# A graph network's output layer: own features through the adjacency's diagonal, division by degree behind the dense product

## The chip, the cores and the metric

The kernel runs on one core of one Trainium2 chip. The metric is the device time of one execution in microseconds. Engines: PE multiplies matrices, DVE is the vector engine, ACT the scalar engine, POOL is GpSimd, SP here only issues DMA.

## The reference, cut to what matters

Four graph layers over x (2708 x 512, fp32) with one adjacency matrix. The third layer multiplies by the adjacency three times ("hops"). The change concerns the end of the third hop and the fourth layer:

```python
deg = max((adj != 0).sum(-1), 1)
...
# fourth layer; node_degree = deg, so dinv * a_hat * dinv divides each row by deg
a_hat  = adj + eye(n)
a_norm = dinv * a_hat * dinv
pooled = a_norm @ x + x
x = layernorm(x + relu(pooled @ W + b))
```

In other words pooled = (adj @ x + x) / deg + x, which equals (adj + diag(1 + deg)) @ x / deg. The division acts on rows and can wait until after the multiplication by W.

## The kernel before

Each hop and the output layer are a "sweep": two ranges of columns, in each seven second-level Strassen products (Q1 to Q7), in each again seven chains of matmuls. DVE forms the sums of adjacency tiles, `comb`, and of features, `tsum`, and adds each finished chain to its result, `leave`. `at(position, f)` puts an action in a list that is sorted by position; the compiled order follows this list only roughly. In the traces a wait at one instruction of POOL holds back those behind it on that engine: POOL starts a layernorm's power at 2876.21 us, 3.67 us after DVE has its input ready (2872.54), behind three DMA issues, the first of them after an idle time of 2.29 us.

```python
for o, x, y, op_, pos in (("s3", (0,0), (1,0), ALU.subtract, -0.5), ((1,0), (1,0), (1,1), ALU.add, 0.6), ...):
    for k in range(nk):                               # sums of adjacency tiles z
        at(b + u * (pos + 0.8 * k / nk), lambda a=(o, x, y, op_, k), f=comb: f(*a))
...
def sums(g):                                          # new features, before the next sweep
    ...
    nc.vector.tensor_tensor(t["T1"], t["T3"], t["B11"], ALU.subtract)
    nc.vector.tensor_tensor(t["T2"], t["B22"], t["T1"], ALU.subtract)
    nc.vector.tensor_tensor(t["T3"], t["B22"], t["T3"], ALU.subtract)
    nc.vector.tensor_tensor(t["T4"], t["B21"], t["T2"], ALU.subtract)
```

At the end of the third hop each row tile is turned to natural layout (four transposes, `ps_n`), normalized and stored, then transposed back (four more, `ps_t`) and stored a second time as X3T:

```python
def b(...):                                           # done5, per row tile
    ps = untranspose2(cc, s, lo, w)
    got["x"] = y = nat("o")
    layernorm([(y, 0, D)], ps, w, True)
    store2(X3, y, h, r0, w)
def c(...):
    store_T(X3T[g, h, s][:, lo : lo + w], transposed([(got["x"], 0, D)], w)[:, :, :w])
```

The output layer loads X3T and a row of 1/deg, and prepares the sum before the dense product:

```python
def pre(s, c):                                        # done6
    nc.vector.tensor_tensor(y, y, t, ALU.add)         # adj @ x + x
    nc.vector.tensor_tensor(y, y, row[g, h, s], ALU.mult)
    nc.vector.tensor_tensor(y, y, t, ALU.add)
...
px = dense(lambda c: cc(s, c)[:, lo : lo + w], W[6], w)
nc.vector.tensor_tensor(px[:w], px[:w], vec[6][:w], ALU.add)
```

The layernorm takes its power on POOL, between two small DVE instructions. In the trace of this kernel, loads that POOL has to issue first delay that power, and DVE stands still behind it (3.84 us in the line shown below).

## Time and profile before

| | |
|---|---|
| time, median of 3 | 2920.15 us (2917.83 to 2923.89) |
| span of the profiled execution | 2921.0 us |
| PE busy | 98% |
| DVE busy | 77% |
| PE's waits from 2430 us on | 12 us, every one for DVE |

The prediction reads these and shows the lines. One more is worth having, of DVE's timeline near the end of the kernel before (start, duration, engine, line, operation, and in brackets the idle time before it and what ended it):

```profile
2876.81 0.15 DVE L555 SCALAR_TENSOR_TENSOR rstd<-mv,rstd 83x1 f32<-83x1 f32 x1 [3.84 <-POOL rstd L553]
```

DVE stands for 3.84 us behind a power on POOL, and PE's hole at 2878.70 follows.

### The profile page before, as it was taken

To read this page: it belongs to the slowest core of one execution; us is meant where nothing else is said; L and a number is where in the kernel's file an instruction comes from. 1 tells how busy PE (TensorE), PEld (TensorE's weight loads), DVE (VectorE), ACT (ScalarE), POOL (GpSimd) and SP (SyncE) were. 2 spreads that over 40 slices of the span, in tenths; PEclk is the share of its full clock that TensorE was granted. 3 is DMA by queue.
4 is the path that set the end of the run, shared out by engine and by line. 5 is a ranking of instruction groups with operands and counts; after the bars stand their busy time and mean duration, and the time that the engine had idled before them with its cause. 6 is when DMAs were issued, how large, how long until landed. Compare 5 with 4: busy or idle time off the path is not lost. (4 is left out here: it accounts for less than half of the span.)

```text
span 2921.0 us, 37394 instructions
## 1 busy us (share of the span) xinstructions
PE 2863.3 (98%) x10846; PEld 1847.0 (63%) x10846; DVE 2235.8 (77%) x5676; ACT 579.0 (20%) x1133; POOL 658.2 (23%) x1178
## 2 busy tenths in 40 slices
PE   7999999999999999999999999999999999999998
PEld 5655665557665656766666666666666666655664
DVE  5898697566638675875789788887888878689887
ACT  4644200101137454651100000000000200100001
POOL 0123224213310101123113033030330413512202
PEclk9999999999999999999999999999999999999999
DMA  7666466445634333665677777576775776966653
GB/s 224 190 211 182 135 212 215 132 154 160 186 107 140 115 114 99 174 190 154 204 203 223 202 206 234 156 217 196 218 223 149 225 204 181 262 164 179 181 162 89
DMA packets 376248, 523.96 MB, mean 179 GB/s; under 512 B 64454, under 2 KB 326640, under 8 KB 376044
## 3 DMA queue, kind: packets, MB, share of 16 engines
q1 hardware_dynamic: 307128, 372.01, 44.4%
q0 software_dynamic: 53376, 139.76, 15.0%
q10 hardware_dynamic: 15540, 9.82, 1.2%
q8 instruction: 86, 1.41, 0.2%
q14 instruction: 118, 0.97, 0.1%
HBM read 432.14 MB, written 89.21 MB: 178 GB/s over the span
## 5 line engine op out<-in xcount | busy, mean ns | idle before, releaser
L1114 DVE TENSOR_TENSOR z<-z 128x339 f32<-128x339 f32 (+1 forms) x966 | 457.0, 504 | 14.8 <-PE accu L1154 3.6
L1172 ACT COPY q<-accu 128x338 f32<-128x338 f32 (+1 forms) x84 | 34.5, 443 | 983.0 <-PE accu L1154 983.0
L1154 PE MATMUL accu<-z,t 128*128 128x338 f32 (+1 forms) x644 | 196.0, 451 | 6.5 <-DVE q L1178 3.5
L1154 PE MATMUL accc<-s,t 128*128 128x338 f32 (+1 forms) x644 | 198.4, 451 | 1.1 <-DVE s L1114 1.1
L1154 PE MATMUL accd<-z,t 128*128 128x338 f32 (+1 forms) x644 | 193.8, 448 | 2.3 <-DVE z L1114 2.3
L1154 PE MATMUL accc<-z,t 128*128 128x338 f32 (+1 forms) x644 | 194.4, 448 | 0.0
L553 POOL TENSOR_TENSOR rstd<-rstd,neg_half 128x1 f32<-128x1 f32 (+3 forms) x92 | 62.1, 675 | 577.7 <-DVE rstd L552 574.7
L1275 POOL DMA_DIRECT2D Y<-y x192 | 104.8, 552 | 372.2 <-DVE y L1270 341.6
L396 DVE TENSOR_TENSOR a<-a,a 128x384 f32<-128x384 f32 (+2 forms) x330 | 161.2, 509 | 16.2 <-PE accu L451 15.7
L1154 PEld LDWEIGHTS accu<-z,t 128*128 128x128 f32 x644 | 122.5, 192 | 68.7 <-DVE q L1178 4.0
L1154 PEld LDWEIGHTS accd<-z,t 128*128 128x128 f32 x644 | 122.2, 190 | 63.5 <-DVE z L1114 2.9
L1154 PEld LDWEIGHTS accc<-s,t 128*128 128x128 f32 x644 | 120.7, 191 | 65.4 <-issue 8.7
L1154 PEld LDWEIGHTS accc<-z,t 128*128 128x128 f32 x644 | 121.9, 190 | 60.7 <-issue 2.1
L1114 DVE TENSOR_TENSOR s<-z 128x338 f32<-128x338 f32 (+1 forms) x322 | 150.2, 504 | 10.6 <-PE accc L1154 7.1
L1178 DVE TENSOR_TENSOR q<-q,accd 128x338 f32<-128x338 f32 (+1 forms) x112 | 56.3, 502 | 128.4 <-PE accd L1154 128.4
L972 ACT ACTIVATE e<-row,neg_s 128x384 f32<-128x384 f32 (+5 forms) x176 | 100.4, 570 | 79.8 <-DVE e L974 24.6
L974 DVE TENSOR_TENSOR e<-e,f 128x384 f32<-128x384 f32 (+5 forms) x176 | 87.3, 504 | 31.1 <-ACT f L973 30.5
L973 ACT ACTIVATE f<-row,neg_s 128x384 f32<-128x384 f32 (+5 forms) x176 | 100.0, 568 | 25.4 <-PE accc L451 5.1
L599 PE MATMUL ps_d<-w,q 128*128 128x512 f32 (+2 forms) x192 | 85.9, 595 | 1.4 <-DVE ld L1360 1.3
L890 DVE SCALAR_TENSOR_TENSOR deg<-a,deg 128x384 f32<-128x384 f32 (+2 forms) x152 | 75.2, 503 | 14.0 <-DMA a<-in_adjT 12.7
L399 POOL DMA_DIRECT2D As<-a x120 | 64.6, 542 | 92.9 <-DVE a L396 77.4
L975 DVE SCALAR_TENSOR_TENSOR a<-a,e 128x384 f32<-128x384 f32 (+2 forms) x160 | 79.9, 505 | 4.2 <-DMA a<-in_adjT 2.2
(609 smaller groups left out, 5933.8 us busy)
## 6 DMA issues: line engine op xcount, KB each, us to landing
z<-As SPq DMA_DIRECT2D x320, 169.5 KB
z<-As SPq DMA_DIRECT2D x320, 169.0 KB
a<-in_adjT SPq DMA_DIRECT2D x240, 192.0 KB
z<-in_adjT SPq DMA_DIRECT2D x240, 169.5 KB
z<-in_adjT SPq DMA_DIRECT2D x240, 169.0 KB
a<-in_adjT SPq DMA_DIRECT2D x120, 165.0 KB
a<-in_adjT SPq DMA_DIRECT2D x112, 128.0 KB
As<-a POOLq DMA_DIRECT2D x60, 192.0 KB, 3.3
```

The costliest lines, as they stand in the source:

```text
L396: nc.vector.tensor_tensor(A[r, dst, k][:, :n], A[r, a, k][:, :n], A[r, b, k][:, :n], op)
L399: nc.gpsimd.dma_start(out=SD[m][k * P : (k + 1) * P, R0 : R0 + n], in_=A[r, dst, k][:, :n])
L553: nc.gpsimd.tensor_tensor(rstd[:w, 1:2], rstd[:w, 0:1], neg_half[:w], ALU.pow)
L599: nc.tensor.matmul(o, lhs(c), r, start=c == 0 and n == 0, stop=c == DC - 1, skip_group_check=True)
L890: nc.vector.scalar_tensor_tensor(d[:w, :n], a[:w, :n], 0.0, d[:w, :n], ALU.not_equal, ALU.add)
L972: nc.scalar.activation(e[:w, :n], row[R0, h][0][:w, :n], AF.Exp, bias=neg_s[:w, t : t + 1])
L973: nc.scalar.activation(f[:w, :n], row[R0, h][1][:w, :n], AF.Exp, bias=neg_s01[:w, t : t + 1])
L974: nc.vector.tensor_tensor(e[:w, :n], e[:w, :n], f[:w, :n], ALU.min)
L975: nc.vector.scalar_tensor_tensor(a[:w, :n], a[:w, :n], 0.0, e[:w, :n], ALU.not_equal, ALU.mult)
L1114: nc.vector.tensor_tensor(d[:, :n], Z[x + (k,)][:, :n], Z[y + (k,)][:, :n], op)
L1154: nc.tensor.matmul(B[home][:, :n], stat(v, k), a[:, :n], start=bool(start and k == 0), stop=k == nk - 1, skip_group_check=True)
L1275: nc.gpsimd.dma_start(out=rows[:, :, f * P : (f + 1) * P], in_=o[32 * f : 32 * (f + 1), : m * P].rearrange("p (b d) -> p b d", d=P))
```

## The change

The intent: don't make, store, load and add the transposed features. Add 1 + deg to the diagonal of the adjacency tiles as they pass through DVE, and divide by deg in the instruction that adds the bias. Cut to its core:

```diff
+    diag = const.tile([P, 4, KT], F32, name="diag")          # 1 + deg, and differences for Strassen's sums
+    rdeg_f = const.tile([P, 24], F32, name="rdeg_f")          # 1/deg by row tile
...
+                def add_diag(p, q, k, ...):
+                    r0, c0 = (q * K2 + k) * P, i0 + p * n
+                    lo, hi = max(r0, c0), min(r0 + P, c0 + n)
+                    if lo < hi:
+                        z = Z[p, q, k][:, lo - c0 : hi - c0]
+                        nc.vector.scalar_tensor_tensor(z, ident[:, lo - r0 : hi - r0], diag[:, d, ...], z,
+                                                       ALU.mult, ALU.add)
+                for p, q, pos in ((0, 0, -0.52), (1, 0, -0.51), (1, 1, 0.59), (0, 1, 4.04)):
+                    for k in range(nk) if on_diag and op != "12" else ():
+                        at(b + u * (pos + 0.8 * k / nk), ...add_diag...)
...   # done5
-            def c(s=s, lo=lo, w=w, got=got):
-                store_T(X3T[g, h, s][:, lo : lo + w], transposed([(got["x"], 0, D)], w)[:, :, :w])
...   # a few small instructions; 16 small loads and one transpose bring 1/deg into rdeg_f
...   # done6: rows(), load_x3T() and pre() removed
-                nc.vector.tensor_tensor(px[:w], px[:w], vec[6][:w], ALU.add)
+                nc.vector.scalar_tensor_tensor(px[:w], px[:w], rdeg_f[:w, r : r + 1], vec[6][:w], ALU.mult, ALU.add)
-            p = p0 - 0.095 + 0.14 * i if end else p0 + 0.4 + 0.25 * i
+            p = p0 - 0.095 + 0.14 * i if end else p0 + 0.1 + 0.28 * i
-    sweep2(S[6], 0, done6)
+    sweep2(S[6], 0, done6, True)
```

More of the change, by code (lines that the diff above doesn't have):

```diff
@@ L102, in gnn_kernel @@
     nc.vector.memset(rdeg, 1.0)
+    diag = const.tile([P, 4, KT], F32, name="diag")
+    nc.vector.memset(diag, 1.0)
+    diag_r = const.tile([P, 3], F32, name="diag_r")
+    nc.vector.memset(diag_r, 0.0)
+    rdeg_f = const.tile([P, 24], F32, name="rdeg_f")
     wab_sb = const.tile([P, 2 * DC, 2], F32, name="wab_sb")
@@ L130, in gnn_kernel @@
            for g, (_, n) in enumerate(RANGES2) for h in range(2)}
-    X3T = {(g, h, s): dram.tile([D, n], F32, name=f"X3T{g}_{h}{s}", tag=f"X3T{g}_{h}{s}")
-           for g, (_, n) in enumerate(RANGES2) for h in range(2) for s in range(2)}
     SUMS = ("s1", "s2", "s3", "s4")
@@ L908, in end @@
                 nc.vector.tensor_scalar(o, ps[:wq, i : i + 1], 1.0, None, ALU.max)
+                nc.vector.tensor_scalar(diag[:wq, h, q : q + 1], o, 1.0, None, ALU.add)
                 nc.vector.reciprocal(o, o)
@@ L1081, in ext_sums, with tiles2, sweep2 @@
             nc.gpsimd.dma_start(out=SE[m, g, s][q * P : (q + 1) * P, :], in_=E[o][:, :n])
-    def sweep2(base, ext, done, extra=None):
+    def tiles2(n):
+        return [(s, lo, min(P, n - lo)) for s in range(2) for lo in range(0, n, P)]
+    def sweep2(base, ext, done, on_diag=False):
         nk = K2 + ext
@@ L1120, in sweep2, with add_diag @@
                         at(b + u * (pos + 0.8 * k / nk), lambda a=(o, x, y, op_, k), f=comb: f(*a))
+                def add_diag(p, q, k, op=op, Z=Z, i0=i0, n=n):
+                    r0, c0 = (q * K2 + k) * P, i0 + p * n
+                    lo, hi = max(r0, c0), min(r0 + P, c0 + n)
+                    if lo < hi:
+                        z = Z[p, q, k][:, lo - c0 : hi - c0]
+                        d = {"11": 0, "22": 1, "s1": 1, "s2": 2, "s3": 0, "s4": 3}[op]
+                        nc.vector.scalar_tensor_tensor(z, ident[:, lo - r0 : hi - r0], diag[:, d, r0 // P : r0 // P + 1],
+                                                       z, ALU.mult, ALU.add)
+                for p, q, pos in ((0, 0, -0.52), (1, 0, -0.51), (1, 1, 0.59), (0, 1, 4.04)):
+                    for k in range(nk) if on_diag and op != "12" else ():
+                        at(b + u * (pos + 0.8 * k / nk), lambda p=p, q=q, k=k, f=add_diag: f(p, q, k))
                 def tsum(nm, x, y, T=T, st=st, nk=nk):
@@ L1204, in cc @@
                         return Q[hi_ if c >= 2 else lo_, s, c % 2]
-                    tiles = [(s, lo, min(P, n - lo)) for s in range(2) for lo in range(0, n, P)]
+                    tiles = tiles2(n)
                     done(b + 2.1, 0.15 if (g, h) != (1, 0) else 0.12, g, i0, n, h, cc, tiles)
@@ L1236, in rest_add, with rest_diag @@
                     nc.vector.tensor_tensor(d[:, :n], d[:, :n], ps[r][:, :n], ALU.add)
+            def rest_diag(h, R=R, i0=i0, n=n):
+                c = NH - KR - (i0 + n)
+                z, z32 = R[h, 1], R[h, 2]
+                for t, rows, i, at_, d in [(z, KA, 0, c, 0)] if h == 0 else [
+                        (z, KA, KR, c, 1), (z32, P, 64, c + KA - KR, 2), (z32, P, 96, c + KA - KR, 2)]:
+                    w = {0: KR, KR: KA - KR}.get(i, 32)
+                    o = t[:rows, at_ : at_ + w]
+                    nc.vector.scalar_tensor_tensor(o, ident[:rows, i : i + w], diag_r[:rows, d : d + 1], o, ALU.mult,
+                                                   ALU.add)
             for j, pos, h, e, to in REST2[g]:
@@ L1241, in sweep2 @@
                     at(b - 1.5 * u, lambda h=h, f=rest_load: f(h))
+                    if on_diag and g == 1:
+                        at(b + u * (pos - 0.2), lambda h=h, f=rest_diag: f(h))
                 ps = []
@@ L1244, in sweep2 @@
                 at(b + u * (pos + 0.6), lambda to=to, f=rest_add, ps=ps: f(ps, to))
-            if extra is not None:
-                extra(base + 14 * g, g, i0, n)
     def untranspose2(cc, s, lo, w):
@@ L1283, in done5, with b @@
         for i, (s, lo, w) in enumerate(tiles):
-            got = {}
             r0 = i0 + s * n + lo
-            def b(s=s, lo=lo, w=w, r0=r0, got=got):
+            def b(s=s, lo=lo, w=w, r0=r0):
                 ps = untranspose2(cc, s, lo, w)
-                got["x"] = y = nat("o")
+                y = nat("o")
                 layernorm([(y, 0, D)], ps, w, True)
                 store2(X3, y, h, r0, w)
-            def c(s=s, lo=lo, w=w, got=got):
-                store_T(X3T[g, h, s][:, lo : lo + w], transposed([(got["x"], 0, D)], w)[:, :, :w])
-            p = p0 + 0.1 + 0.24 * i
-            at(p, b)
-            at(p + 1.1, c)
+            at(p0 + 0.1 + 0.24 * i, b)
     def row_tiles(Y):
@@ L1308, in gnn_kernel, with diag_ends, finish_degrees @@
     next_x2(S[6], X3)
+    def diag_ends():
+        d1, d2 = diag[:, 0, :], diag[:, 1, :]
+        nc.vector.tensor_tensor(diag[:, 2, :], d2, d1, ALU.subtract)
+        nc.vector.tensor_tensor(diag[:, 3, :], d1, d2, ALU.subtract)
+        nc.vector.tensor_copy(diag_r[:KR, 0:1], d1[:KR, KT - 1 :])
+        nc.gpsimd.dma_start(out=diag_r[KR:KA, 1:2], in_=d2[: KA - KR, KT - 1 :])
+        for r in (64, 96):
+            nc.gpsimd.dma_start(out=diag_r[r : r + 32, 2:3], in_=d2[KA - KR : KR, KT - 1 :])
+    at(S[2] + 4.0, diag_ends)
+    def finish_degrees():
+        t = small.tile([24, P], F32, name="fd", bufs=1)
+        nc.vector.memset(t, 1.0)
+        for g, (i0, n) in enumerate(RANGES2):
+            for h in range(2):
+                for s in range(2):
+                    r, a = 12 * g + 6 * h + 3 * s, i0 + s * n
+                    nc.gpsimd.dma_start(out=t[r : r + 2], in_=DROW[h][0, a : a + 2 * P].rearrange("(k i) -> k i", i=P))
+                    nc.gpsimd.dma_start(out=t[r + 2 : r + 3, : n - 2 * P], in_=DROW[h][0:1, a + 2 * P : a + n])
+        ps = bank("ps_r", [P, 24])
+        nc.tensor.transpose(ps, t, ident[:24, :24])
+        nc.scalar.copy(rdeg_f, ps)
+    at(S[3] + 12.0, finish_degrees)
     def start6():
@@ L1317, in done6 @@
     def done6(p0, dp, g, i0, n, h, cc, tiles):
-        def rows(s):
-            row[g, h, s] = ring_tile("row")
-            nc.gpsimd.dma_start(out=row[g, h, s][:, :n], in_=bcast(DROW[h][0:1, i0 + s * n : i0 + (s + 1) * n], n))
-        x3T = {}
         end = (g, h) == (1, 0)
-        def load_x3T(s, c):
-            t = ring_tile("x3T")
-            nc.gpsimd.dma_start(out=t[:, :n], in_=X3T[g, h, s][c * P : (c + 1) * P, :])
-            x3T[s, c] = t
-        def pre(s, c):
-            t = x3T[s, c]
-            y = cc(s, c)
-            nc.vector.tensor_tensor(y[:, :n], y[:, :n], t[:, :n], ALU.add)
-            nc.vector.tensor_tensor(y[:, :n], y[:, :n], row[g, h, s][:, :n], ALU.mult)
-            nc.vector.tensor_tensor(y[:, :n], y[:, :n], t[:, :n], ALU.add)
-        for s in range(2):
-            at(p0 - (1.9 if end else 0.6), lambda s=s: rows(s))
-            for c in range(DC):
-                if end:
-                    a = p0 - 1.8 + 0.05 * c
-                    b = p0 - 1.5 + 0.2 * (c - 2) + 0.4 * s if c >= 2 else p0 + {
-                        (1, 1): -0.9, (1, 0): -0.6, (0, 1): -0.3, (0, 0): -0.07}[s, c]
-                else:
-                    a, b = p0 - 0.5 + 0.4 * s + 0.05 * c, p0 + 0.4 * s + 0.05 * c
-                at(a, lambda s=s, c=c: load_x3T(s, c))
-                at(b, lambda s=s, c=c: pre(s, c), True)
         for i, (s, lo, w) in enumerate(tiles[3:] + tiles[:3] if end else tiles):
@@ L1358, in b @@
                 y = got["x"]
-                nc.vector.tensor_tensor(px[:w], px[:w], vec[6][:w], ALU.add)
+                r = 12 * g + 6 * h + 3 * s + lo // P
+                nc.vector.scalar_tensor_tensor(px[:w], px[:w], rdeg_f[:w, r : r + 1], vec[6][:w], ALU.mult, ALU.add)
                 nc.vector.scalar_tensor_tensor(y[:w], px[:w], 0.0, y[:w], ALU.max, ALU.add)
```

## The prediction

Of the single durations that the prediction quotes from the trace, 272 ns is the record of a transpose, 504 ns that of a DVE sum of 128x339, and 5.3 us the median of the 256 KB stores of the transposed features from issue to landing. The ten matmuls after the 3.48 us hole, which took 4.53 us, ran at a granted clock of 0.69 (2878.70 to 2883.30 us); it was 1.00 ahead of the hole (2870 to 2875).

> **What bounds the kernel now.** I read the page first, for the engine that fills the span.
>
> ```profile
> span 2921.0 us, 37394 instructions
> PE 2863.3 (98%) x10846; PEld 1847.0 (63%) x10846; DVE 2235.8 (77%) x5676; ACT 579.0 (20%) x1133; POOL 658.2 (23%) x1178
> ```
>
> PE is busy for 2863 of 2921 us, so the kernel is as long as PE's list of instructions plus 58 us of holes. Anything taken off another engine is worth only the hole that it closes. The change touches the last two sweeps (the third hop, which ends near 2545 us, and the output layer after it), so I then cut that stretch into windows and asked for PE's waits in it.
>
> ```profile
> core 0: us, PE busy (x) PEld busy (x) DVE busy (x) ACT busy (x) POOL busy (x), PEclk, DMA share, GB/s
> 2278.00:2535.00 257.00, 256.84 (x1030) 173.59 (x1029) 198.23 (x489) 31.42 (x54) 89.23 (x149) 1.00 0.72 210
> 2540.00:2580.00 40.00, 33.25 (x112) 20.37 (x111) 33.00 (x67) 3.38 (x8) 11.20 (x21) 1.00 0.80 211
> 2580.00:2860.00 280.00, 278.45 (x946) 167.52 (x945) 242.00 (x582) 18.75 (x31) 50.59 (x88) 1.00 0.59 170
> 2860.00:2893.00 33.00, 29.21 (x91) 17.23 (x90) 24.21 (x60) 2.44 (x3) 12.90 (x24) 0.95 0.40 120
> 2893.00:2921.00 28.00, 20.49 (x48) 8.16 (x46) 18.38 (x43) 4.88 (x6) 3.29 (x6) 0.91 0.14 50
> ```
>
> PE is solid while the features are transposed (first row), loses 6.75 us where the output layer starts, 1.55 in its body, 3.8 just before its end; the last row is the closing dense products. What those holes wait for:
>
> ```profile
> PE accd L1154 <- DVE z L1114: 3.8, 3, 2.3
> PE accu L1154 <- DVE q L1178: 3.5, 1, 3.5
> PE accu L1154 <- DVE z L1114: 3.0, 1, 3.0
> PE ps_d L599 <- DVE ld L1360: 1.3, 1, 1.3
> ```
>
> Always DVE, never directly a DMA. The timeline of DVE shows why it is late at the start of the layer:
>
> ```profile
> 2541.68 0.43 DVE L1135 TENSOR_TENSOR t<-B11D,B11B 128x256 f32<-128x256 f32 x1 [5.20 <-PE accc L1154]
> 2549.66 0.51 DVE L1178 TENSOR_TENSOR q<-q,accu 128x338 f32<-128x338 f32 x1 [3.77 <-ACT q L1172]
> ```
>
> DVE stood idle for 5.20 us until a block of the new features was loaded (the releaser named is the one that came last; I take it to be the load of B11D), then 3.77 us for a copy by ACT, and had to catch up afterwards, at PE's cost. The 3.5 us hole near the end begins on POOL:
>
> ```profile
> 2874.59 0.54 POOL L145 DMA_DIRECT2D ld<-X  x1 [2.29 <-DMA z<-in_adjT]
> 2875.13 0.56 POOL L1328 DMA_DIRECT2D x3T<-X3T  x1
> 2875.68 0.51 POOL L147 DMA_DIRECT2D ld<-X  x1
> 2876.21 0.56 POOL L553 TENSOR_TENSOR rstd<-rstd,neg_half 83x1 f32<-83x1 f32 x1
> ...
> 2878.70 4.53 PE L1154 MATMUL accu<-z,t 128*128 128x339 f32 x10 [3.48 <-DVE q L1178]
> ```
>
> POOL's list is served in order: DMA issues hold up the small power of a layernorm, that holds up DVE, and DVE holds up PE's accumulator.
>
> [...] The trace has 272 ns for a record, but that is latency: by start times four take 0.43 us (2278.22 to 2278.65). [...] here the ten records after the 3.48 us gap took 4.53 us where ten take 3.01 elsewhere. [...] the trace has 504; successive starts are only 0.42 us apart, which is what a busy DVE pays. [...] the trace's median is 5.3 us[...].
>
> **The change part by part.**
>
> 1. *The transposed features are no longer made.* 24 row tiles lose 4 transposes each, 96 of PE's records. A tile of 128 rows costs 0.43 us, one of 82 or 83 rows 0.28 (2285.22 to 2285.50). 16 x 0.43 + 8 x 0.28 = 9.2 us, in a window where PE has 0.16 us of holes. All of it should come off the time.
> 2. *24 copies on ACT and 24 stores on POOL go with them.* The copies sat idle 34.1 us in total for their buffer (its store not landed); that is how a copy of an accumulator got stuck behind them for DVE's 3.77 us. I expect this wait gone, and the 5.20 us wait shortened by one or two us, as 5.6 MB of stores leave a stretch where the DMA share reaches 1.06 (2540 to 2560). DVE should have caught up by 4 to 6 us, so of the 6.6 us of PE's waits here some 2 remain: gain 4.5.
> 3. *96 DVE instructions in the output layer go* (32 each of adding, scaling, adding): 96 x 0.42 = 40 us of DVE. This is not PE's path except where DVE is behind: the 1.3 us wait and small ones of 0.2. Gain 1.5.
> 4. *32 loads of the transposed features and 8 of the degree rows go from POOL and free 40 buffers of the ring.* At the 3.5 us hole only two such issues (1.1 us) stand between; the loads of the row tiles, which wait for their buffer, stay. The hole should halve, and the clock's 1.5 us partly with it: gain 2.5.
> 5. *Diagonal terms are added to adjacency tiles.* By the index ranges 7 pieces in the first column range and 6 in the second for each of 6 products, 78, plus 4 for the remaining rows. DVE's 384 and 256 column instructions start 0.47 and 0.33 us apart, so one of 128 columns should take about 0.20 (an estimate from those two). 82 x 0.20 = 16 us of DVE, against the 40 taken away. Each stands just ahead of a subtraction of the same tile, which waits for the same load, so there is no new wait; but six stand in the first product, where DVE is behind: cost 1.
> 6. *Division by degree* merges into the addition of the bias: one instruction of PSUM for another, 0.69 us each. Nothing.
> 7. *Preparations*: 22 tiny DVE operations in the second layer, seven small ones in the third, and in the middle of the first hop 16 small DMAs (about 0.55 us each on POOL, idle there) and one transpose on PE. If PE came to it early, it would wait; I charge 1.
> 8. *The end.* Closing dense products start at 2892.62, some 0.3 us after the last matmul could have let them; then PE and the layernorm chain both step by 3.4 us a tile. Gain 0.3. Dense products elsewhere start a little earlier, and their inputs are ready since nothing follows the sums.
>
> Sum: 9.2 + 4.5 + 1.5 + 2.5 - 1 - 1 + 0.3 = 16 us. Predicted 2920.15 - 16 = 2904 us, 0.55% less.
>
> **The rivals.** (a) DVE is the real limit of the output layer, and 40 us less of it shows in full. Against: between 2580 and 2860 PE has 1.55 us of holes in 280. This rival would give about 2870. (b) The diagonal additions delay the tiles that PE is about to use, and PE waits for DVE at the head of many products. For: every hole here is a wait for DVE. Against: DVE is at 242 of 280 us and gets lighter on balance. If each of 12 products lost 0.5 us, the time would be 2910. (c) The transpose of the degrees blocks PE: 16 issues of 0.55 us and a landing are some 12 us[...]. For: memory set, loads and transpose are written in one place. Against: the trace shows neighbouring pieces of code interleaved on each engine (steps of one layernorm lie between other instructions), so the list is ordered by when inputs should be ready. It would make 2912 to 2916. (d) The boundary hole is due to the loading of features alone and stays as long: 2908.
>
> **Range and chances.** The 9.2 us are nearly certain; the other 7 depend on who waits for whom, and a changed instruction order can move holes elsewhere by a few us (there are 40 us of holes outside this stretch). Predicted 2904, eight in ten between 2897 and 2913. Both 2% limits lie far off: even with every hole of the two sweeps closed, some 25 us, the gain is 0.9%. Chances: faster 0.01, same 0.98, slower 0.01.
>
> **What would show it.** Right: no transposes of the third hop's output, PE's busy time about 9 us less, DVE's about 25 us less by records (96 x 0.505 away, 82 x 0.28 added), PE's waits between 2530 and 2570 at 2 to 3 us instead of 6.6, the hole before the last product under 2 us. Wrong: PE waiting for a diagonal tile (step 5), for the degrees' transpose (step 7), or a boundary hole unchanged (step 2); a saving above 25 us would mean that PE's list shrank by more than I count, or that holes before 2270 us closed for reasons that I have not seen.

## The result, and the profile after

The changed kernel gave a correct result in 2902.05 us (median of 4 runs, 2900.68 to 2905.18), beside 2920.24 us for the kernel before in the same rounds. The ratio of the two is 0.9938, 95% interval 0.9921 to 0.9955. Here and below a ratio is the mean time of one kernel's runs over that of the other's runs of the same rounds, so it is not quite the ratio of the quoted medians. 2904 us had been predicted.

The head of the page after:

```profile
span 2898.6 us, 37074 instructions
PE 2844.5 (98%) x10751; PEld 1831.7 (63%) x10751; DVE 2217.3 (76%) x5690; ACT 567.4 (20%) x1110; POOL 626.1 (22%) x1133
```

PE is busy 18.8 us less. That is more than the transposes' 9.2; the slow matmuls behind before's long hole are part of it (1.5 us by the prediction's count, at the granted clock of 0.69), and part is scatter: between the repeated traces of both kernels (experiments 1 and 5) it is 12.3 us (2859.8 less 2847.5). DVE is busy 18.5 us less, where some 25 were predicted from the lengths of records. Records overlap (a DVE sum of 128x339 has a record of 0.504 us, and the next starts 0.42 us after it), and busy time counts an overlap once: the 96 operations are worth 38.4 us of it (experiment 6: 2255.7 less 2217.3) and the 82 additions 15.9 (experiment 4: 2217.3 less 2201.4), which step 5 had put at 16. That leaves 22.5; the longer fused division (24 x 0.06 us) and the 22 tiny operations on the degrees (2.0 us) take most of the rest. The windows of roughly the same stages as in the prediction's table (the ruler below cuts them exactly):

```profile
core 0: us, PE busy (x) PEld busy (x) DVE busy (x) ACT busy (x) POOL busy (x), PEclk, DMA share, GB/s
2278.00:2530.00 252.00, 247.72 (x931) 164.49 (x930) 195.37 (x484) 20.31 (x34) 71.19 (x127) 1.00 0.67 201
2530.00:2570.00 40.00, 36.42 (x130) 22.80 (x130) 39.92 (x89) 1.67 (x4) 7.82 (x15) 1.00 0.63 178
2570.00:2840.00 270.00, 270.00 (x913) 162.52 (x912) 222.33 (x560) 19.58 (x32) 34.21 (x60) 1.00 0.53 155
2840.00:2868.00 28.00, 28.00 (x94) 17.45 (x93) 15.51 (x37) 1.63 (x2) 6.92 (x12) 1.00 0.24 71
2868.00:2899.00 31.00, 19.92 (x47) 7.96 (x45) 15.34 (x36) 4.88 (x6) 3.30 (x6) 0.88 0.13 45
```

The third and fourth rows are the output layer: its body and its end now have no hole at all. But the first row, solid before, loses 4.3 us, the second still 3.6, and the last row is 31 us long where it had been 28. PE's waits from 2430 us to the end (total, times, longest):

```profile
PE accd L1178 <- DVE z L1125: 3.7, 3, 1.5
PE accu L1178 <- DVE z L1125: 2.3, 1, 2.3
PE ps_n L1285 <- DVE q L1202: 1.8, 1, 1.8
```

All of these lie at the boundary between the hop and the output layer. DVE's timeline there:

```profile
2474.76 0.35 DVE L1139 SCALAR_TENSOR_TENSOR z<-ident,diag,z 128x128 f32<-128x128 f32 x1 [0.51 <-DMA z<-As]
2475.41 0.30 DVE L1139 SCALAR_TENSOR_TENSOR z<-ident,diag,z 128x82 f32<-128x82 f32 x1 [0.30 <-DMA z<-As]
2480.04 0.27 DVE L1139 SCALAR_TENSOR_TENSOR z<-ident,diag,z 128x46 f32<-128x46 f32 x1 [3.91 <-DMA z<-As]
...
2481.33 0.50 DVE L1125 TENSOR_TENSOR s<-z 128x338 f32<-128x338 f32 x1
...
2527.91 0.43 DVE L1159 TENSOR_TENSOR t<-B11D,B11B 128x256 f32<-128x256 f32 x1 [2.73 <-DMA B11D<-X]
```

DVE's wait of 3.77 us for ACT is gone. In its place DVE stands 3.91 us at a new instruction, the diagonal of a tile that is not loaded yet, with the first subtraction of that product (`s<-z`) behind it.

**A ruler for all traces.** Executions differ by some microseconds in stages that the change does not touch, so I cut each span at four products that every kernel has, by the start of their first matmul: A, from the start to the fifth product (T1) of the third hop's first range; B, to the first product of the output layer; C, to its fourth product (T2), which is past the boundary's holes; D, to the closing dense products; E, from there to the end of the span. Microseconds:

| trace | A | B | C | D | E | B to E |
|---|---|---|---|---|---|---|
| before | 2229.7 | 273.9 | 73.7 | 315.3 | 28.4 | 691.3 |
| before, repeated | 2220.5 | 273.9 | 72.1 | 315.3 | 28.4 | 689.7 |
| after | 2220.0 | 269.3 | 70.7 | 307.1 | 31.4 | 678.5 |
| after, repeated | 2224.2 | 269.8 | 70.8 | 307.1 | 31.4 | 679.1 |

B, D and E repeat to half a microsecond or better. B to E is 11.6 us shorter (the means are 690.5 and 678.8): B gains 4.3, C 2.1, D 8.2, and E gives 3.0 back. A scatters by 9 us.

### The profile page after: what moved, and what is told of

Its sections match the earlier page's. It is cut to its first block, busy times and chain, and to the rows that moved or that the text cites.

```text
span 2898.6 us, 37074 instructions
## 1 busy us (share of the span) xinstructions
PE 2844.5 (98%) x10751; PEld 1831.7 (63%) x10751; DVE 2217.3 (76%) x5690; ACT 567.4 (20%) x1110; POOL 626.1 (22%) x1133
## 5 line engine op out<-in xcount | busy, mean ns | idle before, releaser
L1125 DVE TENSOR_TENSOR z<-z 128x339 f32<-128x339 f32 (+1 forms) x966 | 455.1, 503 | 12.3 <-PE accu L1178 3.8
```

The lines of the kernel that those rows point to most:

```text
L1125: nc.vector.tensor_tensor(d[:, :n], Z[x + (k,)][:, :n], Z[y + (k,)][:, :n], op)
```

## The experiments

**1. The kernel before, repeated** (a control; no edit).

> The kernel before, unchanged, as a control. In the two traces the layers before the first hop, whose instruction lists for PE are the same in both kernels, differ by 8 us (first matmul of the first hop's remaining rows at 1470.3 us before, 1462.2 after). Theory: that is chance of the single profiled run, so this run is within 0.15% of the kernel before, and its landmark falls anywhere between 1460 and 1472. Rival: the change itself speeds up the early layers, so the landmark stays within 1 us of 1470.

Measured: 2916.52 us against 2916.03 for the other copy; ratio 0.9997 (0.9984 to 1.001). Its trace gives the second row of the table; the landmark of the expectation fell at 1466.2 us, so the 8 us between the first two traces need not come from the change. Differences of 3 us can be read in B to E, but not from a few timed runs.

**2. The kernel before without the second set of transposes.** The load reads another array of that size, so the result is wrong.

```diff
             at(p, b)
-            at(p + 1.1, c)
...
-            nc.gpsimd.dma_start(out=t[:, :n], in_=X3T[g, h, s][c * P : (c + 1) * P, :])
+            nc.gpsimd.dma_start(out=t[:, :n], in_=X2T[g, h][c * P : (c + 1) * P, s * n : (s + 1) * n])
```

> The kernel before without the making of transposed features (96 PE transposes, 24 copies, 24 stores); the output layer's loads read another tensor of the same layout instead, so the result is wrong on purpose. Everything else of the kernel before stays. Theory (steps 1 and 2): 9 us from PE's list and some 2 us from the wait for ACT at the start of the output layer, 10 to 12 us less than before, about 2909. Rival: the copies and stores matter more than the transposes: 14 us or more. Other rival: holes take their place and under 6 us are gained.

Measured: 2910.06 us, ratio 0.9976 (0.9963 to 0.999); B 266.6, C 69.9, D 315.3, E 32.8. B falls by 7.2 us. Of the 24 tiles 18 lie in B; by the prediction's durations they make 6.8. C falls by 3.0, of which the six tiles left are 2.3. So the transposes' price is right. The boundary's holes did not close as I had expected; PE's timeline there:

```profile
2524.36 3.08 PE L1154 MATMUL accu<-z,t 128*128 128x338 f32 x10 [0.45 <-DVE z L1114]
2532.54 2.10 PE L1154 MATMUL accd<-z,B21C 128*128 128x338 f32 x6 [2.26 <-DVE z L1114]
2550.72 2.15 PE L1154 MATMUL accu<-z,t 128*128 128x338 f32 x4 [1.87 <-DVE z L1114]
```

That is 4.6 us without copies and stores, the same sum as in the repeated run of before (1.61 + 3.00). DVE's wait for ACT is gone from this trace, and the boundary is as open as before; DVE's wait for B11D is 4.44 us. And E grew by 4.4 us, which took much of the gain: by the clock it is 6 to 7 us, between the theory and the second rival.

**3. The changed kernel with the transposes back on PE,** without copy and store.

```diff
+            def c(w=w, got=got):
+                ps = bank("ps_t", [P, DC, P])
+                for c_ in range(DC):
+                    nc.tensor.transpose(ps[:, c_, :w], got["x"][:w, c_ * P : (c_ + 1) * P], ident[:w, :w])
+
             at(p0 + 0.1 + 0.24 * i, b)
+            at(p0 + 0.1 + 0.24 * i + 1.1, c)
```

> The changed kernel with the 96 transposes put back on PE alone: no copy, no store, result right. Theory (step 1): PE has no holes to hide them, so 9 us slower than the changed kernel, about 2911. Rival: transposes alone cost little because PE waits anyway for features in that stretch (4 us of new holes there): under 5 us.

Measured: correct, 2908.24 us, ratio 0.9973 (0.9961 to 0.9986). B 275.6, C 69.0, D 307.1, E 31.4: against the mean of the two traces of after, B is 6.1 longer, C 1.7 shorter. With the transposes PE comes later to the boundary, and DVE is ready for it more often. So they cost 4.3 us net here, less than the 9.2 us that they occupy and as the rival had it, though the timed ratio (0.9973 against 0.9938) looked like the full amount.

**4. The changed kernel without the diagonal additions** (wrong result).

```diff
-    sweep2(S[6], 0, done6, True)
+    sweep2(S[6], 0, done6)
```

> The changed kernel without the 82 diagonal additions (wrong on purpose). Theory (step 5): they cost at most 1 to 2 us, so 2900 to 2902. Rival: they cause the new holes of the last hop's end (DVE waited 3.9 us at a diagonal addition for a tile's load, then PE lost 1.0 and 1.8 us) and lengthen the hole at the start of the output layer: without them 4 us or more less, under 2898.

Measured: 2898.4 us, ratio 0.9937 (0.9925 to 0.995). By the clock that is the first reading of after (0.9938), and I could have closed the matter there. The ruler says otherwise: B 268.1, C 67.0, D 307.1, E 31.4. B is 1.5 us and C 3.8 us shorter than with the diagonal. Of PE's waits between 2470 and 2640 us one is left:

```profile
PE accu L1178 <- DVE z L1125: 1.9, 1, 1.9
```

So the diagonal costs up to 5.3 us, all near the boundary and none in D. The 3.8 us in C are sure: the six traces with the diagonal, with the sums in their place and without transposes (the two of after, 6, 7, 9 and 10) have 70.2 to 71.0. The 1.5 us in B are less so: these six and experiment 8 have 268.1 to 269.8 there.

**5. The changed kernel, repeated** (a control; no edit).

> The changed kernel itself, with the same instructions, as the measure for the other three in the same rounds. Both theories: 2900 to 2905 us, 0.994 of the kernel before, and the same lengths of the same stretches as in its first trace: last layer's first second-level piece to the closing dense product 70.8 us, and no hole in the output layer's body.

Measured: correct, 2904.9 us against 2918.12 for before; ratio 0.9952 (0.9939 to 0.9964). The fourth row of the table; the 70.8 us of the expectation is C.

**6. The changed kernel with as many DVE instructions as the old preparation had,** at their old places, without loads.

```diff
+        def pre(s, c):
+            y = cc(s, c)
+            for _ in range(3):
+                nc.vector.tensor_tensor(y[:, :n], y[:, :n], y[:, :n], ALU.max)
+        ...                                    # at the old positions
-            p = p0 - 0.095 + 0.14 * i if end else p0 + 0.1 + 0.28 * i
+            p = p0 - 0.095 + 0.14 * i if end else p0 + 0.4 + 0.25 * i
```

> The changed kernel with the 96 small VectorE operations put back where the old preparation stood (three maxima of a tile with itself, in place, which leave the result as it is), but without the 40 loads on GpSimd. The output layer from the first finished tile to the closing dense product took 315.3 us in each trace with the preparation and 307.1 in each without: 8.2 us. Theory: these 8.2 us were the layernorm waiting behind GpSimd's loads, so this kernel keeps them: within 2 us of the changed kernel, and the stretch at 307 to 309. Rival: VectorE's extra operations themselves held the layernorm up: then the stretch is back at 313 to 315 and the kernel 6 to 8 us slower than the changed one.

Measured: correct, 2904.78 us, ratio 0.9953 (0.9941 to 0.9966); D 310.1, between the two expectations. The edit also moves the dense products back to their old places; experiment 7 does so too and has 0.4 us, so that is the most they can account for unless the loads hid it. PE's holes in D stand where the old body had its two, now of one microsecond each:

```profile
2619.96 1.40 PE L1249 MATMUL accr<-r,B11R 116*128 116x338 f32 x4 [0.95 <-DVE q L1260]
2629.58 3.70 PE L605 MATMUL ps_d<-w,q 128*128 128x512 f32 x8 [0.97 <-DVE ld L1400]
```

**7. The changed kernel with the 40 loads on POOL and the old places of the dense products,** nothing reading them.

```diff
+        def load_x3T(s, c):
+            t = ring_tile("x3T")
+            nc.gpsimd.dma_start(out=t[:, :n], in_=X2T[g, h][c * P : (c + 1) * P, s * n : (s + 1) * n])
+        ...                                    # rows(s) as before; at the old positions
-            p = p0 - 0.095 + 0.14 * i if end else p0 + 0.1 + 0.28 * i
+            p = p0 - 0.095 + 0.14 * i if end else p0 + 0.4 + 0.25 * i
```

> The changed kernel with the 32 tile loads and 8 row loads put back on GpSimd's queue and into the shared ring, at the old positions; nothing reads them. Theory: the stretch of the output layer is back at 313 to 315 us, with a hole of some 4 us just before the closing dense product and 1 to 2 us in the body, and the kernel is 5 to 8 us slower than the changed one (2906 to 2911). Rival (VectorE's operations were the cause): the stretch stays at 307 to 309 and the time within 2 us of the changed kernel.

Measured: correct, 2907.88 us, ratio 0.9961 (0.9948 to 0.9973); D 307.5, but E 34.7. My theory of the output layer's end falls: 40 loads alone bring no hole back. The 3 us that this kernel is slower by come after the last product (see 10).

**8. The changed kernel with the last layer's sums T3 and T4 put off** until shortly before their products.

```diff
-            nc.vector.tensor_tensor(t["T3"], t["B22"], t["T3"], ALU.subtract)
-            nc.vector.tensor_tensor(t["T4"], t["B21"], t["T2"], ALU.subtract)
...
+            if base == S[6]:                   # the other layers as before
+                at(base + 7.8 + 0.3 * i, lambda g=g: late[g][0](), True)    # T3
+                at(base + 10.2 + 0.3 * i, lambda g=g: late[g][1](), True)   # T4
```

> The changed kernel with the last layer's two sums T3 and T4 put off until the product needs them, so that VectorE has two operations less per group in front of the first evictions at the boundary of the layer. Theory: the hole of about 5 us that is left at that boundary is VectorE's queue of sums, so 2 to 4 us of it go and the kernel is 2 to 4 us faster than the changed one. Rival: it is the chain of the last hop's tiles through store and load, which this does not shorten: the holes add up to 4.5 us or more as before, and the time is within 1 us.

Measured: correct, 2900.45 us, ratio 0.9939 (0.9926 to 0.9953), 4.5 us by the medians ahead of the repeated after in the same rounds, though the intervals overlap. The ruler is firmer: C falls from 70.8 to 66.9 (B 268.1, D 307.9, E 31.4; B to E 674.3 against 679.1). PE's holes at the boundary went from five, 7.8 us in the first trace of after (2480 to 2560 us), to two:

```profile
2495.51 0.63 PE L1299 MATMUL ps_n<-ident,q 128*128 128x128 f32 x4 [1.83 <-DVE q L1216]
2532.22 2.25 PE L1192 MATMUL accd<-z,B21C 128*128 128x338 f32 x6 [2.01 <-DVE z L1139]
```

What DVE had to catch up with was its own queue of sums: in this trace DVE still waits 3.16 us for the load of B11D, and yet C is as short as without the diagonal. So the hole in C takes both, the additions that make DVE late and the sums that it then finds in its queue; no run removes both. By B to E this is the shortest correct kernel; its timed ratio does not set it apart from the first reading of after (0.9938).

**9. Loads and preparation together,** as they were, on top of the changed kernel.

```diff
+        def pre(s, c):
+            nc.vector.tensor_tensor(y[:, :n], y[:, :n], t[:, :n], ALU.add)
+            nc.vector.tensor_tensor(y[:, :n], y[:, :n], row3[s][:, :n], ALU.mult)
+            nc.vector.tensor_tensor(y[:, :n], y[:, :n], t[:, :n], ALU.add)
+        ...                                    # rows, load_x3T and pre at the old positions
```

> The changed kernel with loads and preparation put back together as they were: 32 tile loads and 8 row loads through the shared ring, and the 96 VectorE operations that read them, their results unused. Each half alone gave back little of the 8.2 us that the output layer gained (from the second half's T2 product at the layer's boundary to the closing dense product: 307.1 us in the changed kernel, 307.5 with the loads alone, 310.1 with the operations alone, 315.3 before). Theory: it is the two coupled, VectorE standing in order behind a load that comes late, and this kernel is back at 313 to 316 with the hole of 4 to 6 us ahead of the closing dense product, some 6 to 9 us slower in that stretch than the changed kernel. Rival: the halves add and the rest comes from something else in the change (where the degrees are applied, the store of the transposed features): then 310 to 311.

Measured: 2913.35 us, ratio 0.998 (0.9967 to 0.9993); D 313.9, E 35.0. The result is wrong: contrary to what I wrote, the operations work in place on the layer's sums, so their results are used. Their cost is what mattered. D comes back by 6.8 us, 0.4 for the loads, 3.1 for the operations and 3.3 that only the two together have. The holes near the end of D (the two of one microsecond in the body are there as in 6, and one of 0.47):

```profile
2862.08 3.12 PE L1178 MATMUL accu<-z,t 128*128 128x339 f32 x10 [0.96 <-DVE q L1202]
2871.37 1.68 PE L1178 MATMUL accd<-z,B21D 128*128 128x339 f32 x4 [0.83 <-DVE z L1125]
```

These are two small holes, where before had one of 3.5 us. All five add up to 4.2 us while D grew by 6.8, so the starts of fixed products say more than the holes do. D stays 1.4 us under that of before; I put this down to a different order of instructions around it, which no run isolates.

**10. The changed kernel with 25 small instructions more on POOL.**

```diff
+    def pad():
+        t = small.tile([P, 1], F32, name="pad", bufs=1)
+        for _ in range(25):
+            nc.gpsimd.memset(t, 0.0)
+    at(S[3] + 6.0, pad, True)
```

> The changed kernel with 25 one-column memsets of an unused tile on GpSimd, two thirds into the run, so that its list has as many entries as that of the kernel before (905). GpSimd's last drain took 3.85 us in both traces before, 6.87 in seven traces of the changed kernel and its variants, 10.14 with 40 loads added, 8.26 in the kernel before without the preparation; each time the same in the same program. Theory: its length depends on how many instructions GpSimd's list has, so it comes out at another value here, 3.9 if the count alone decides, and the time from the closing dense product to the end of the span goes from 31.4 to about 28.4 us. Rival: it depends on what GpSimd did (loads, stores), and it stays 6.87 with 31.4 us to the end. Time otherwise as the changed kernel.

Measured: correct, 2903.38 us, ratio 0.9946 (0.9935 to 0.9958); E 31.7. What ends the span after is not the last transfer but a closing instruction of POOL. The lines (durations of the shortest, median and longest in ns, first start to last start in us) in the kernel before, after, with 40 loads (7), and here:

```profile
L1420 POOLq DRAIN  x3: 51/106/3850, 2916.3 to 2920.7; - x3
```

```profile
L1447 POOLq DRAIN  x3: 46/106/6872, 2890.9 to 2898.3; - x3
```

```profile
L1464 POOLq DRAIN  x3: 46/102/10140, 2894.7 to 2905.3; - x3
```

```profile
L1454 POOLq DRAIN  x3: 46/102/6872, 2890.4 to 2898.0; - x3
```

SP, which issues the stores of the output, closes with drains of its own, before and after:

```profile
L1420 SPq DRAIN  x3: 7/7/7, 2920.1 to 2920.5; - x3
```

```profile
L1447 SPq DRAIN  x3: 7/7/7, 2894.7 to 2898.0; - x3
```

Before, POOL's long drain ends at 2920.2, just as SP gets there; after, at 2897.8, when SP has been there for 3 us. In the two kernels traced twice POOL's repeats to 2 ns. The count of instructions does not set it: the 25 left it at 6.872. The 40 loads added 3.27 us, in both kernels that have them (7 and 9), some 0.08 us each. That cannot be the whole rule, since the kernel before has such loads too and shows the shortest, 3.85, and experiment 2, with as many loads and no stores of X3T, shows 8.26 (experiment 11 has 6.52). What does set it stays open; that it lengthened E by 3.0 us is shown.

**11. An attempt at a better kernel:** the sums put off in all sweeps of this schedule, and one more small product of the layernorm on POOL.

```diff
+            nm = small.tile([P, 1], F32, name="nm")
+            nc.vector.tensor_scalar(nm[:w], mv[:w, 0:1], -1.0, None, ALU.mult)
...
-            nc.vector.scalar_tensor_tensor(rstd[:w, 0:1], mv[:w, 0:1], -1.0, rstd[:w, 1:2], ALU.mult, ALU.mult)
+            nc.gpsimd.tensor_tensor(rstd[:w, 0:1], nm[:w], rstd[:w, 1:2], ALU.mult)
```

> An attempt to beat both kernels: the changed kernel with the two sums put off in every sweep that has this schedule, and the product of mean and 1/deviation of the layernorm moved from VectorE to GpSimd, so that VectorE does not stand behind GpSimd's power. The late sums alone brought 4 us. Theory: the move takes VectorE's waits for the power (17 us in 23 waits in the output layer) away and the holes that are left at the boundary of the layer with them; 2895 to 2899 us, 0.991 to 0.993 of the kernel before. Rival: TensorE does not wait for these, since the output layer's body has no hole; then as the late sums alone, 0.994.

Measured: correct, 2934.56 us, ratio 1.0054 (1.004 to 1.0068): slower than either kernel, and both expectations missed. A is 2238.2, C 72.3, D 315.2. In A, long before the layers that I had in mind, PE's waits for ACT grew from the first of these lines (after, repeated) to the second:

```profile
PE cnt L656 <- ACT mask L646: 4.8, 8, 2.0
```

```profile
PE cnt L673 <- ACT mask L663: 21.2, 10, 15.7
```

The layernorm's helper is shared with earlier layers. I read this as ACT standing in order behind a product that POOL serves late; since two things were changed at once, no run separates them.

## Why the prediction was right or wrong

The time was right within 2 us. But the traces account for 11.6 us in B to E, not 16, and the terms came out as follows (negative is a gain; the prediction's steps 1, 2 and 5 meet in B and C).

| step | predicted | measured | from |
|---|---|---|---|
| 1 transposes | -9.2 | -9 alone, about -4 net | 2, 3 |
| 2 copies, stores, boundary | -4.5 | -3.6 without the diagonal | 4 |
| 3 and 4, preparation and loads | -1.5 - 2.5 | -8.2 | D of the table |
| 5 diagonal | +1 | +3.8 to +5.3 | 4 |
| 6 division | 0 | +0.2 | below |
| 7 preparations | +1 | not seen | below |
| 8 the end | -0.3 | +3.0 | 10 |

**Step 1** was priced rightly (its sum, 16 x 0.43 + 8 x 0.28, is 9.1 and not 9.2): 72 transposes in B are worth 7.2 us, 0.10 us each. Wrong was "all of it should come off the time": it assumed that the window stays free of holes. PE, freed of the transposes, arrives earlier at the boundary and waits there. Even without the diagonal, B gains 5.8 and not 7.2; in all traces of the changed kernel PE waits 1.24 or 1.25 us (2.53 in experiment 11) in B before it turns a tile to natural layout, until ACT has normalized an earlier one (the trace names ACT's instruction; through which buffer PE waits for it is not shown); in before it came late enough.

**Step 2.** The 3.77 us wait for ACT went, as said. The 5.20 us wait became 2.73, but not because the load came earlier: B11D arrived 38.1 us after the layer's first product started before (2541.68 less 2503.6), 38.6 after (2527.91 less 2489.3). DVE came later to it. The gain appears once the diagonal is out: C falls from 72.9 (mean of the two before) to 67.0, of which 2.3 are transposes. The cause named, the copies and stores, is not supported by experiment 2, where they are gone, DVE's wait for ACT too, and 4.6 us of holes stay. It is not ruled out either: experiment 3 has the transposes on PE without copies and stores, and its C is 69.0 us beside 72.9, but it carries the rest of the change as well. The sign that the prediction named, PE's waits between 2530 and 2570 us at 2 to 3 us, did not come: those behind the first product add up to 5.0 us after (1.49 + 2.31 + 1.24). Experiment 8 shows another remedy, DVE's sums.

**Steps 3 and 4** were too small by half. The body's 1.5 us and more came with the DVE instructions alone (3.1); for the rest it took loads and preparation together. The prediction added the two as if they were separate. My reading is that DVE has to be both busy and held up before PE feels it: waits of DVE for POOL's power are nearly as long in total in the kernel with loads alone (19.2 us in D) as before (20.0), and PE has no hole. But with both (experiment 9) they are 15.1 us, so their total alone does not tell; which of them PE feels is not shown. The hole near the end was misread in part: only one load of the transposed features, 0.56 us, stands between the two small DVE instructions there (2872.40 and 2876.81); POOL itself stood idle for 2.29 us ahead of a load of the row tiles.

**Step 5** is the part that failed most plainly: "so there is no new wait". The reason given was that each addition stands just ahead of a subtraction of the same tile. In the compiled order the additions of the first product stand in a group ahead of all its subtractions, so DVE waited 3.91 us for the last tile of the group before it could begin with the first. The trace without the diagonal has the first `s<-z` at 256.2 us after the end of A, the one with it at 261.3 (2477.24 less 2221.07, 2481.33 less 2220.03):

```profile
2477.24 0.50 DVE L1125 TENSOR_TENSOR s<-z 128x338 f32<-128x338 f32 x1
```

The size of the instructions was not the trouble: 0.22 to 0.35 us by records, and 0.19 us each of DVE's busy time, as estimated. This was rival (b), and it was to be 6 us spread over twelve products; it is 4 to 5 us at one boundary.

**Step 6** is nearly nothing. The fused instruction takes longer, and as the closing tiles follow one another in a chain, the powers on POOL start 3.46 and 3.48 us apart (2880.55, 2884.01, 2887.49) where they had been 3.40 and 3.42 apart (2906.16, 2909.56, 2912.98). Over four tiles 0.2 us is an estimate from these:

```profile
L1359 DVE TENSOR_TENSOR ps_d<-ps_d,vec x24: 686/690/697, 2641.7 to 2913.6; 128x512 f32<-128x512 f32 x16, 82x512 f32<-82x512 f32 x4, 83x512 f32<-83x512 f32 x4
```

```profile
L1386 DVE SCALAR_TENSOR_TENSOR ps_d<-ps_d,rdeg_f,vec x24: 747/752/760, 2616.4 to 2888.1; 128x512 f32<-128x512 f32 x16, 82x512 f32<-82x512 f32 x4, 83x512 f32<-83x512 f32 x4
```

**Step 7.** Rival (c) falls: the transpose of the degrees stands in PE's list where its data had long been there, without a wait:

```profile
1552.06 0.24 PE L1360 MATMUL ps_r<-ident,fd 24*128 24x24 f32 x1
```

**Step 8** missed what happens after the last tile: the prediction looked at PE and the layernorm, and the end of the span is POOL's.

Rival (a) falls too: 40 us less of DVE's work gave 8.2 us in D. Rival (d) is half true: with the diagonal in, C gained 2.1 us, no more than its transposes; without it, 5.9.

So a gain near the predicted 16 us came out of -8.2 where -4 was expected, and of costs of some 5 and 3.0 us where next to none was: errors of both signs that cancelled, which is luck. That the timed gain (ratios 0.9938, 0.9952 and, with the harmless memsets, 0.9946: 14 to 18 us) lies above the 11.6 of the traces would need 2 to 6 us in A. There nine traces with the change have 2220.0 to 2224.2 (experiment 11 left out), the three without have 2220.5, 2226.1 and 2229.7. Whether A gained anything stays open.

## What to carry to other kernels

Where PE is full, price what is removed from its list exactly, and then ask where PE arrives earlier and whom it finds unready there; here PE, freed of 7.2 us in B, gained only 5.8 without the diagonal and 4.3 with it. A small instruction can cost its engine what the load costs that it waits for (here 3.91 us of waiting for one of 0.27 us): before placing one "next to" its consumer, look where the compiled order puts it. When timed runs differ by less than their scatter, cut the traces at landmarks that all kernels share; a 4 us effect was plain there which the medians hid.
